# A graph layer on one Trainium2 core: one PSUM tile of two banks becomes two tiles of one bank each

## The chip, the cores and the metric

The kernel runs on one core of one Trainium2 chip. A core has five engines with an instruction queue each, and every queue is worked off in order: PE multiplies matrices (its weight loads are shown apart as PEld), DVE and ACT work element by element, POOL computes little here and issues the gathers, SP issues the other transfers. PE writes its results into PSUM, and DVE and ACT read and write there too. PSUM is divided into banks; the kernel counts a bank as 512 numbers of 32 bits in each of 128 partitions (P * G), and its PSUM tiles take eight banks in all. The engines wait for each other through semaphores. The metric is the time of one execution on the device in microseconds (us), as the median of several runs.

## What is computed

There are 12500 nodes of 128 features and 412500 edges, sorted by `dst`, one of them a loop from each node to itself.

```
theta = x[dst] - x[src]
w = sigmoid(relu(theta @ W1 + b1) @ W2 + b2)          # the gate: one number for each edge
agg = segment_sum(w * theta, dst)
indeg = segment_sum(1, dst)
out = layernorm(x + agg + indeg * (x @ W4 + b4))
```

## The kernel before, in words

**Table.** Since theta @ W1 is a difference of two rows of x @ W1, the kernel first makes a table `z` in device memory that holds x @ W1 and x for every node (`table_chunk`, lines 745 to 767). Each of 13 chunks has up to eight tiles of 128 nodes, worked in two halves of G = 4 tiles. For a half, PE transposes four tiles into PSUM (L754), ACT copies them to SBUF (L757), PE multiplies them by W1 (L760), ACT copies the product into the staged rows (L763). One PSUM tile `px` of two banks, from `wide()` (L737), takes both halves of a chunk, each half in a bank of its own.

**Parts.** The edges are worked in 276 parts of up to 1024 edges and more. Two parts make a block with one window of destination nodes. Parts from 18 on (PLAIN) run in a loop whose order is written out by hand for PE, DVE and ACT (`part`, under `manual_schedule`). For each part:

- POOL gathers the rows of `z` with eight indirect transfers (L395) into one of six buffers `zbuf`. The gather of part s + 3 is held until a matmul of part s - 1 is done, so at most some three parts lie ahead.
- PE spreads the rows of the destinations by a one-hot product into a PSUM tile `y` (L885, two buffers).
- DVE subtracts (L943), applies relu and W2 (L948), sums to the logits (L954) and makes one-hots (L918, L1122).
- ACT turns the logits into gates: L970 writes them into PSUM, L976 into SBUF. DVE weighs half of the rows with them at the start of the next part (L998), ACT weighs the other half (L1005).
- PE sums the weighed rows by destination (L1140). Every second part the sums of a block are completed (L1205) and normalised (L1233 to L1258).
- Edges whose source lies in 32 ranges of "hot" rows go another way: PE takes their rows from tables that stay in SBUF (L1059), makes their logits (L1086, L1087, L1100, the last into PSUM) and transposes them (L1103), ACT makes their gates and weighs them (L1092, L1109, L1112).

**Placement.** The lists of 64 parts (a set) are prepared during the parts before them, mostly on DVE. `place` (L498 to L709) is a generator of small steps, and `spend` gives each part a few of them, at the end of the part's DVE work. Named by what they do, they are: the start of a set (L527 to L545), 32 rounds of picking maxima (L573 to L580, all in SBUF), the hot list (L606, L612), four scans (L633 to L654), nine shifts (L671 to L674), and the end, which transposes the lists on PE and copies them on ACT (L694, L701, L705). The starts, hot lists, scans, shifts and ends need a PSUM scratch of up to one bank. One set is made before the loop and four in it; the last of these has only two parts, but its steps are the same.

**The tile that the change touches.** In the loop, one tile `px` of two banks lives from part 17 to the end. At part 17 it is cut in two by slices of one bank, `halves` (L1368, L1369): `halves[0]` is the placement's scratch, `halves[1]` holds the gates (`gate`, written by L970, read by L998), the hot edges' logits (`lgh`, written by L1100, read by L1109) and a node's own term (`own`, written by L1215, read and written by L1233). The kernel's language derives the semaphore waits from accesses to tiles. The same name `px` is used ahead of the loop for small tiles of `bases` (L432) and `first_turned` (L472), and for the placement's scratch while the first set is made.

Of the kernel before, what the change touches and what calls it, by code (L numbers as in the profile page):

```python
# [9 lines left out]
F32 = mybir.dt.float32  # L10
# [4 lines left out]
AF = mybir.ActivationFunctionType  # L15
# [5 lines left out]
P = 128  # L21
# [11 lines left out]
G = 4  # L33
# [49 lines left out]
def gnn_resnorm(  # L83
# [37 lines left out]
    nc = tc.nc  # L121
# [16 lines left out]
    while n0 < N:  # L138
        t = max(1, (N - n0) // P)
# [105 lines left out]
    ident = wni[:, 1, :]  # L245
# [35 lines left out]
    for i, t in enumerate(terms):  # L281
        at = slice(i * HALF // 2, i * HALF // 2 + 1)
# [141 lines left out]
    def bases(c0, c1, ps):  # L424

        b0, b1_ = c0 // SUB, c1 // SUB
        nc.vector.tensor_scalar(base_b[:, b0:b1_], base_r[:, c0:c1:SUB], float(N - WB), None,
                                op0=OP.min)
        nc.vector.tensor_scalar(first_b[:, c0:c1], base_r[:, c0:c1], float(N - SW), None,
                                op0=OP.min)  # L430
        nc.vector.tensor_copy(base_f[:, c0:c1], base_r[:, c0:c1])
        pb = ps.tile([P, 2 * P * G], F32, name="px")[:, :c1 - c0]  # L432
        nc.tensor.matmul(pb, ones_r, base_f[:, c0:c1], start=True, stop=True)
        first = first_c[:, c0:c1]
        nc.vector.tensor_copy(first, pb)
        for h in range(SUB):
            nc.vector.tensor_scalar(base_c[:, b0:b1_, h], first[:, ::SUB],
                                    float(N - WB), None, op0=OP.min)
        nc.vector.tensor_scalar(first, first, float(N - SW), None, op0=OP.min)
        lo = max(b0, 1)  # L440
        nc.vector.tensor_sub(step_c[:, lo:b1_], base_c[:, lo:b1_, 0], base_c[:, lo - 1:b1_ - 1, 0])
# [26 lines left out]
    def first_turned(t, ps):  # L468
        n = t.shape[0]
        f = turn_f[:n]  # L470
        nc.scalar.activation(f, t, AF.Copy)
        pt = ps.tile([P, 2 * P * G], F32, name="px")[:, :n]  # L472
        nc.tensor.transpose(pt, f, ident[:n, :n])
        return pt.rearrange("p (s k) -> p k s", k=K)

# [235 lines left out]
    with tc.manual_schedule(engines={SP}), tc.tile_pool(name="work", bufs=2) as wp, tc.tile_pool(  # L711
        name="ps_y", bufs=2, space=bass.MemoryType.PSUM
    ) as ps_y, tc.tile_pool(
        name="ps_l", bufs=1, space=bass.MemoryType.PSUM
# [7 lines left out]
        def next_xT():  # L722
            xTs.append(xT_buf[len(xTs) % len(xT_buf)])
            return xTs[-1]
# [5 lines left out]
        def y_tile():  # L730

            turn_y[0] += 1
            if turn_y[0] % 3 == 0:
                return pz.rearrange("p (g d) -> p g d", d=D)
            return ps_y.tile([P, G, D], F32, name="y")

        def wide():  # L737

            return ps_l.tile([P, 2 * P * G], F32, name="px")

        def turning():

# [2 lines left out]
        def table_chunk(c, xt):  # L745

            n0, np_, m = chunks[c]
            zt = staged[c % len(staged)]
            px = wide().rearrange("p (t e) -> p t e", e=P)
            for g0 in range(0, m, G):  # L750
                at = slice(g0, min(g0 + G, m))
                g = at.stop - g0
                for j in range(g0, at.stop):
                    pe = nc.tensor.transpose(px[:, j, :np_], xt[:np_, j, :], ident[:np_, :np_])  # L754
                table_steps.append(pe)
                xT = next_xT()
                nc.scalar.activation(xT[:, :g, :np_], px[:, at, :np_], AF.Copy)  # L757
                py = y_tile()[:np_, :g]
                for j in range(g):
                    pe = nc.tensor.matmul(py[:, j, :], xT[:, j, :np_], wts[:, 0, :],  # L760
                                          start=True, stop=True)
                table_steps.append(pe)
                nc.scalar.activation(zt[:np_, at, :D], py, AF.Copy)  # L763
            act = nc.scalar.activation(zt[:np_, :m, D:], xt[:np_, :m, :], AF.Copy)
            nc.sync.dma_start(
                z[n0:n0 + np_ * m, :].rearrange("(p t) d -> p t d", t=m), zt[:np_, :m, :])
            return pe, act
# [190 lines left out]
        halves = []  # L958
# [66 lines left out]
        def hot_load(f):  # L1025

            i0, g, i1, i = f
            a = i0
            while a < i1:
                (hot_s, _, n), j = hot_set(a)  # L1030
                m = min(i1 - a, n - j)
                nc.sync.dma_start(
                    hot_src[:, i % NU, (a - i0) * EP:(a - i0 + m) * EP],
                    hot_s[g, j:j + m].rearrange("(o p) l e -> o (p l e)", o=1).to_broadcast([P, m * EP]))
                a += m
# [40 lines left out]
        def tables():  # L1076

            for r in range(0, HR, RG):
                nc.sync.dma_start(
                    tabs[:, r:r + RG], x[r * HOT:(r + RG) * HOT, :].rearrange(  # L1080
                        "(r p t) d -> p r t d", p=P, t=HT))

        def hot_turned(t):

            xT = xT_all[:, (t - PLAIN) % HX, :]
            nc.tensor.matmul(pz, wneg, xT, start=True, stop=False)  # L1086
            nc.tensor.matmul(pz, y_of(t), blocks[t // SUB]["oh"][:, BP:], start=False, stop=True)  # L1087
# [174 lines left out]
        def fetch(b):  # L1262
            if b < NK:
                load_block(b)
# [73 lines left out]
        def spend(kinds, most=NS):  # L1338

            while most and credit[0] > 0 and steps[0] is not None and steps[1] in kinds:  # L1340
                credit[0] -= cost[steps[1]]
                advance(kinds)
                most -= 1

        def early_part(s):

            b, h = divmod(s, SUB)
            if s == 8:
                tables()
            credit[0] = min(credit[0] + 5.5, 5.5) if s < PLAIN - 5 else 200.0  # L1350
            if s == PLAIN - 4:
                credit[0] = 200.0
                spend("kspmcz")
                assert steps[0] is None
                credit[0] = 0.0
            for f in firsts.get(s, []) + [f for f in rest_of if max(f[0] - 7, PLAIN - 4) == s]:
                hot_load(f)
            if h == 0:
                if b + 2 >= NY:
                    fetch(b + 2)  # L1360
                if NY <= b + 1 < W0:
                    window(b + 1)
            elif b and b + 3 < PLAIN // SUB:
                load_dst(b + 3)
            while opened:
                hot_out(*opened.pop(0))
            if s == PLAIN - 1:
                px = wide()  # L1368
                halves.extend(px[:, i * P * G:(i + 1) * P * G] for i in range(2))  # L1369
                hot_turned(PLAIN)  # L1370
                hot_relu(PLAIN)
            if h and b:
                total(b - 1)
                own(b - 1)
            spend("c")
            logits(s)
            ends.append(newest[0])
            if s >= NH + 4:
                paced[s + AHEAD] = ends[-3]
            if s + AHEAD >= NH:  # L1380
                gather(s + AHEAD)
            if s + 1 < NH:
                parts[s + 1]["y"] = []
                spread_x(s + 1, 0, copied.pop())
                xT = copy_x(turn_x(s + 1, J))
                if s:
                    add_up(s - 1)
                spread_x(s + 1, J, xT)
                if s + 2 < NH:
                    px = turn_x(s + 2, 0)  # L1390
            else:
                for t in range(s + 1, s + 2 if s + 1 < PLAIN else s + 3):
                    spread_y(t)
                add_up(s - 1)
            if tiled:
                products_of_tiles()
            advance("p")
            gate_sums(s)
            weigh(s)
            if s + 2 < NH:  # L1400
                copied.append(copy_x(px))
            if s == PLAIN - 2:
                one_hot(PLAIN // SUB)
            if s == PLAIN - 1:
                one_hot(PLAIN // SUB + 1, 0, BP)
            if h:
                shift(b)
            if h == 0 and b > 1:
                normalize(b - 2)
            spend("ksmz")  # L1410
            if h == 0 and b + 1 < PLAIN // SUB:
                plain_one_hots(b + 1)
            if s - (PLAIN - 9) in range(len(OPENING)):
                tiles_of(groups[s - (PLAIN - 9)])
            fetch_step(s)
            if s == PLAIN - 1:
                hot_rows(PLAIN)
                hot_weights(PLAIN)

        ends = []  # L1420
        groups, firsts, i = [], {}, 0
# [118 lines left out]
    with tc.tile_pool(name="post_ps", bufs=1, space=bass.MemoryType.PSUM) as pps:  # L1540
        one = const.tile([P, 1], F32, name="one")
        nc.vector.tensor_reduce(one, bad, AX.X, OP.max)
        pb = pps.tile([P, P], F32, name="pb2")
# [193 lines left out]
```

## Time and profile before

| | |
|---|---|
| median of 3 runs (lowest to highest) | 3171.1 us (3168.46 to 3186.73) |
| the profiled execution's own time | 3168.71 us |
| its span, first to last instruction | 3166.6 us |
| PE, weight loads, DVE, ACT, POOL busy | 86%, 72%, 77%, 77%, 68% of the span |
| mean granted clock of PE | 0.889 |
| instructions | 53729 |

The profile is of one execution. A row of instructions gives the start in us from the start of the span, the time, the engine, the line of the kernel, the tile written and the tiles read, their shapes, and in brackets how long the engine had stood idle before it and what ended that. The waits are also given in sums: an engine and line, whom it waited for, us in total, how often, and the longest. A row of windows gives for a stretch of time its length, the busy time of each engine (with the number of instructions), the granted clock of PE (PEclk, 1.00 is full), the busy share of the DMA engines and GB/s.

### The profile page before, as it was taken

How to read it: one execution, taken by the hardware profiler on the slowest of the kernel's cores; microseconds unless marked ns; L12 is line 12 of the kernel's file. 1: busy time of each engine (PE TensorE's matmuls, PEld its weight loads, DVE VectorE, ACT ScalarE, POOL GpSimd, SP SyncE). 2: the span in 40 equal slices, each digit the busy share in tenths (PEclk: the TensorE clock that was granted, in tenths of full speed). 3: DMA queues.
4: the chain of work that ended last, by engine and by line, in shares of the span. 5: the costliest groups of instructions: out<-in, count | busy, mean ns of one | idle time of the engine just before them, and what ended most of it. 6: DMA issues, size and time to landing. Idle time of an engine off the chain costs nothing.

```text
span 3166.6 us, 53729 instructions
## 1 busy us (share of the span) xinstructions
PE 2736.3 (86%) x16422; PEld 2294.6 (72%) x16422; DVE 2435.9 (77%) x4150; ACT 2441.9 (77%) x6397; POOL 2157.0 (68%) x2213
## 2 busy tenths in 40 slices
PE   6868899998878999988798999888898999888797
PEld 5657677777767777767686777777677777777676
DVE  7998689887757988877557898877567888877555
ACT  5446888887767888876778898876787888877685
POOL 3674677777656777776566777776576777775573
PEclk7868899988888999988888999988898999988898
DMA  7564445554444555544354555454354555543342
GB/s 249 157 175 113 115 135 135 137 137 133 116 114 112 138 135 135 137 133 119 103 135 117 137 140 137 134 137 117 102 141 113 138 137 137 135 132 109 101 130 63
DMA packets 239303, 413.23 MB, mean 130 GB/s; under 512 B 63423, under 2 KB 147226, under 8 KB 237470
## 3 DMA queue, kind: packets, MB, share of 16 engines
q0 software_dynamic: 105280, 286.93, 33.0%
q1 hardware_dynamic: 131756, 116.40, 13.9%
q10 hardware_dynamic: 1970, 6.40, 0.6%
q8 instruction: 131, 2.15, 0.3%
q14 instruction: 166, 1.36, 0.1%
HBM read 388.57 MB, written 20.94 MB: 129 GB/s over the span
## 4 chain that ended last, share of the span: by engine, by line


## 5 line engine op out<-in xcount | busy, mean ns | idle before, releaser
L395 POOL DMA_INDIRECT zbuf<-z,src_i x2060 | 2007.3, 974 | 868.5 <-issue 385.4
L1059 PE MATMUL pd<-of,tabs 128*128 128x128 f32 (+2 forms) x4240 | 620.9, 310 | 0.0
L885 PEld LDWEIGHTS y<-y,oh 128*128 128x128 f32 (+1 forms) x2108 | 297.6, 212 | 426.1 <-DVE zbuf L943 359.5
L1059 PEld LDWEIGHTS pd<-of,tabs 128*128 128x128 f32 x4240 | 601.6, 227 | 0.0
L885 PE MATMUL y<-y,oh 128*128 128x128 f32 (+1 forms) x2108 | 328.8, 305 | 253.5 <-DVE zbuf L943 246.4
L1140 PE MATMUL pa<-wx,ow 128*104 128x260 f32 (+1 forms) x2284 | 534.9, 380 | 1.8 <-DVE wx L998 1.8
L1140 PEld LDWEIGHTS pa<-wx,ow 128*104 128x104 f32 x2284 | 369.6, 176 | 80.5 <-issue 2.9
L1092 ACT ACTIVATE hr<-pz 128x512 f32<-128x512 f32 x258 | 153.8, 596 | 314.7 <-PE pz L1087 314.6
L1100 PE MATMUL px<-w_c,hr 128*128 128x1 f32 x2064 | 302.5, 268 | 63.5 <-ACT hr L1092 58.9
L1100 PEld LDWEIGHTS px<-w_c,hr 128*128 128x128 f32 x2064 | 295.3, 220 | 79.5 <-ACT hr L1092 74.0
L1043 ACT ACTIVATE of<-hot_src,nodes 128x512 f32<-128x512 f16 (+2 forms) x530 | 344.4, 697 | 7.0 <-PE pd L1059 3.1
L948 DVE SCALAR_TENSOR_TENSOR zbuf<-zbuf,fix 128x1024 f32<-128x1024 f32 x273 | 331.6, 1215 | 9.3
L1112 ACT ACTIVATE wxh<-pz,wxh 128x128 f32<-128x128 f32 x1032 | 294.4, 368 | 53.0 <-PE pz L1103 48.4
L954 DVE TENSOR_REDUCE lg<-zbuf 128x8 f32<-128x1024 f32 x273 | 329.7, 1208 | 5.0
L1005 ACT ACTIVATE wx<-zbuf,wx 128x128 f32<-128x128 f32 x1028 | 328.7, 390 | 0.0
L943 DVE TENSOR_TENSOR zbuf<-y,zbuf 128x1024 f32<-128x1024 f32 x258 | 313.5, 1215 | 12.3 <-DMA zbuf<-z,src_i 12.2
L1045 ACT ACTIVATE of<-of 128x1024 f32<-128x1024 f32 (+1 forms) x265 | 274.2, 1035 | 8.4
L998 DVE TENSOR_TENSOR wx<-zbuf,px 128x512 f32<-128x512 f32 x258 | 175.9, 682 | 122.2 <-ACT px L970 60.1
L1086 PE MATMUL pz<-xT,wni 128*128 128x512 f32 x516 | 266.7, 599 | 1.1 <-ACT wxh L1112 1.1
L1087 PE MATMUL pz<-oh,y 128*128 128x512 f32 x516 | 267.2, 600 | 0.2 <-ACT oh L865 0.2
L1140 PE MATMUL pa<-wxh,owh 128*104 128x130 f32 x2064 | 262.2, 281 | 0.0
L1140 PEld LDWEIGHTS pa<-wxh,owh 128*104 128x104 f32 x2064 | 252.2, 178 | 0.0
(302 smaller groups left out, 4034.6 us busy)
## 6 DMA issues: line engine op xcount, KB each, us to landing
to_all<-off_d SPq DMA_DIRECT2D x258, 128.0 KB
zbuf<-z,src_i POOLq DMA_INDIRECT x2060
hot_src<-hot_s SPq DMA_DIRECT2D x228, 128.0 KB
z<-zbuf SPq DMA_DIRECT2D x10, 1024.0 KB
y<-z SPq DMA_DIRECT2D x270, 28.0 KB
xw<-in_x_dram SPq DMA_DIRECT2D x138, 52.0 KB
out_dram<-o SPq DMA_DIRECT2D x138, 52.0 KB
wx<-in_x_dram ACTq DMA_DIRECT2D x12, 512.0 KB
```

What stands on the lines that cost most here:

```text
L395: ins = nc.gpsimd.indirect_dma_start(out=rows_of(s)[:, k, :], out_offset=None, in_=z if s >= NH else x, in_offset=IndirectOffsetOnAxis(ap= ...
L885: nc.tensor.matmul(y[:, j, :], d["oh"][:, (k0 + j) * P:(k0 + j + 1) * P], y_of(s), start=True, stop=True)
L943: nc.vector.tensor_sub(half, yy.to_broadcast([P, 2, n, D]), half)
L948: nc.vector.scalar_tensor_tensor(h[:, at, :], h[:, at, :], 0.0, w2.to_broadcast([P, n, D]), op0=OP.max, op1=OP.mult)
L954: nc.vector.tensor_reduce(lg[:, at, 0], h[:, at, :], AX.X, OP.add)
L1005: nc.scalar.activation(wx[:, k, :D], rows_of(s)[:, k, D:], AF.Copy, scale=wx[:, k, D:D + 1])
L1043: nc.scalar.activation(of[:, t, :], hot_src[:, i % NU, :w], AF.Abs, bias=nodes[:, t:t + 1])
L1045: nc.scalar.activation(of, of, AF.Relu, scale=-1.0, bias=1.0)
L1059: newest[0] = nc.tensor.matmul(to[:, q], tabs[:, g * RG + q, t, :], of[:, t, q], start=t == 0, stop=t == HT - 1)
L1100: nc.tensor.matmul(lgh()[:, t % SUB, q:q + 1], hr[:, at], w2_c, start=True, stop=True)
L1112: nc.scalar.activation(wx[:, q, :D], pz[:, q * P:(q + 1) * P], AF.Copy, scale=wx[:, q, D:D + 1])
L1140: newest[0] = nc.tensor.matmul(to if len(w.shape) == 3 else to[:, 0, :], one, w, start=first and i == 0, stop=last and i == len(terms) - 1)
```

## The change

`px` is now a tile of one bank with two buffers, so the tiles take eight banks as before. In a table chunk each half takes its own tile, and in the loop the scratch and the gates' bank are two tiles. The small tiles of `bases` and `first_turned` follow.

```diff
@@ bases
-        pb = ps.tile([P, 2 * P * G], F32, name="px")[:, :c1 - c0]
+        pb = ps.tile([P, P * G], F32, name="px", bufs=2)[:, :c1 - c0]
@@ first_turned
-        pt = ps.tile([P, 2 * P * G], F32, name="px")[:, :n]
+        pt = ps.tile([P, P * G], F32, name="px", bufs=2)[:, :n]
@@ wide
-            return ps_l.tile([P, 2 * P * G], F32, name="px")
+            return ps_l.tile([P, P * G], F32, name="px", bufs=2)
@@ table_chunk
-            px = wide().rearrange("p (t e) -> p t e", e=P)
             for g0 in range(0, m, G):
+                px = wide().rearrange("p (t e) -> p t e", e=P)
                 at = slice(g0, min(g0 + G, m))
                 g = at.stop - g0
                 for j in range(g0, at.stop):
-                    pe = nc.tensor.transpose(px[:, j, :np_], xt[:np_, j, :], ident[:np_, :np_])
+                    pe = nc.tensor.transpose(px[:, j - g0, :np_], xt[:np_, j, :], ident[:np_, :np_])
                 table_steps.append(pe)
                 xT = next_xT()
-                nc.scalar.activation(xT[:, :g, :np_], px[:, at, :np_], AF.Copy)
+                nc.scalar.activation(xT[:, :g, :np_], px[:, :g, :np_], AF.Copy)
@@ early_part
             if s == PLAIN - 1:
-                px = wide()
-                halves.extend(px[:, i * P * G:(i + 1) * P * G] for i in range(2))
+                halves.extend(wide() for _ in range(2))
```

No instruction is added or removed. In the built programs the orders on POOL and SP are the same; on PE, DVE and ACT they differ only in the table and in the first set's placement, up to part 17, and agree from there to the end. What differs in the loop is which semaphores an instruction waits for. Before, the first scratch instruction of a scan or shift (L637 or L671) waits for the latest L1100 and L970, and L1233 or L998 behind an end of a set waits for L701 and L705. After, these waits are gone, and L998 or L1233 carries the wait for L1100 and L970 itself.

## The prediction

> **What bounds the kernel now.** I read the sums of waits first, since no engine is busy all the time, then windows of one block (two parts) in different stretches, then the rows of single parts. The windows show two kinds of block. The first row is a block while maxima are picked (only SBUF is used, I call it a picking block), the second a block while shifts are made (their scratch is in PSUM, a shifting block).
>
> ```profile
> 1142.00:1161.00 19.00, 17.98 (x121) 14.77 (x121) 17.99 (x30) 17.05 (x47) 14.43 (x16) 1.00 0.53 141
> 861.10:886.00 24.90, 20.79 (x113) 17.94 (x112) 18.56 (x31) 16.97 (x45) 15.13 (x16) 0.79 0.42 112
> ```
>
> A picking block takes some 18.9 us: PE is busy 17.98, DVE 17.99, ACT 17.05 of 19.0, so three engines together are its bound. A shifting block gives DVE almost the same work, 18.56, and takes about 24.9. PE's busy time is longer there only because its granted clock is 0.79 and not 1.00. So some 6 us of such a block are waits. The DVE rows of that block say which:
>
> ```profile
> 865.22 0.28 DVE L1205 TENSOR_TENSOR a<-a,pa 104x130 f32<-104x130 f32 x1
> 869.06 0.69 DVE L671 TENSOR_SCALAR px<-et 128x512 int32<-128x512 int32 x1 [3.55 <-ACT px L970]
> ...
> 872.16 0.45 DVE L674 COPY_PREDICATED ew<-px,et 128x255 f32<-128x255 int32 x1
> ...
> 874.02 0.68 DVE L998 TENSOR_TENSOR wx<-zbuf,px 128x512 f32<-128x512 f32 x1
> ...
> 881.85 0.69 DVE L671 TENSOR_SCALAR px<-ew 128x512 int32<-128x512 int32 x1 [2.20 <-ACT px L970]
> ```
>
> DVE has nothing to do until L970 has written the gates; only then comes the shift, 3.5 us (869.06 to 872.6), and only after it the weighing L998 and the next part's L943, for which PE's L885 waits (its tile `y` must be free). So the shift lies in a ring: L943, PE's L885 to L1103, ACT's L1109 to L970, shift, L998, L943. The shift writes the scratch and reads no gate. The wait for L970 comes from the common tile, not from data. In a picking block the same place holds 3.1 us of SBUF work that waits for nothing and runs while PE and ACT do their part of the ring.
>
> The idle PE costs more than the idle time:
>
> ```profile
> 2801.34 1.05 PE L885 MATMUL y<-y,oh 128*128 128x128 f32 x8
> ...
> 2803.58 1.95 PE L1059 MATMUL pd<-of,tabs 128*128 128x128 f32 x16
> ...
> 2813.70 2.07 PE L885 MATMUL y<-y,oh 128*128 128x128 f32 x8 [4.30 <-DVE zbuf L943]
> ...
> 2818.02 3.04 PE L1059 MATMUL pd<-of,tabs 128*128 128x128 f32 x16
> ```
>
> After 4.30 us of idling eight matmuls take 2.07 instead of 1.05 us, and sixteen later ones 3.04 instead of 1.95.
>
> **The change part by part.** Nothing is computed more or less, no transfer or gather is added, moved or resized, and the queues of SP and POOL keep their order. What changes is waits, in three places, and the order of the table.
>
> *(a) The scratch no longer waits for the gates.* The sums of DVE's waits give the price:
>
> ```profile
> DVE px L671 <- ACT px L970: 92.4, 33, 3.8
> DVE px L637 <- ACT px L970: 25.3, 11, 2.9
> DVE px L639 <- ACT px L970: 4.6, 4, 1.4
> ```
>
> A shift has 3.5 us of work to fill a wait of 2.8 us (92.4 / 33); only the longest, 3.8, leave 0.3 us over, for some 16 of the 33 (one per block): 92.4 - 16 x 0.3 = about 88. A scan has more than its wait behind L637:
>
> ```profile
> 2806.68 0.16 DVE L637 COPY px<-col 128x1 f32<-128x1 f32 x1 [2.93 <-ACT px L970]
> ...
> 2810.19 0.36 DVE L654 SCALAR_TENSOR_TENSOR ed<-ew,ed 128x192 int32<-128x192 int32 x1
> ```
>
> That is 3.9 us for a wait of 2.93, so 25.3 + 4.6 = 30 go whole (L639 still has to wait for the hot list's L612, which comes before L970 in ACT's order). Sum: 118. L998 and L1233 take over the wait for L970 as their own; behind them in DVE's queue stands L943, and for that PE's L885. What is late next: in the odd part L1233, which really reads what ACT's L1215 wrote, then PE and DVE together as in a picking block.
>
> As a second way, the four stretches with scans and shifts (7.5 blocks each), and a block in which ACT also makes the square root of the normalisation (every fifth):
>
> ```profile
> 727.90:911.30 183.40, 156.26 (x881) 134.88 (x882) 136.09 (x249) 130.85 (x340) 121.97 (x129) 0.83 0.46 124
> ...
> 2761.30:2947.80 186.50, 157.13 (x877) 135.79 (x878) 137.34 (x257) 129.41 (x340) 123.67 (x130) 0.83 0.44 122
> sum 735.60, PE 624.70 PEld 539.01 DVE 545.51 ACT 519.49 POOL 493.53; mean PE 156.18 PEld 134.75 DVE 136.38 ACT 129.87 POOL 123.38
> ```
>
> ```profile
> 1123.10:1146.70 23.60, 20.98 (x119) 17.72 (x118) 17.03 (x28) 20.07 (x50) 17.81 (x20) 0.86 0.50 136
> ```
>
> If DVE keeps its 136.4 and idles 1.0 per block as in the picking block (19.0 - 17.99), and 1.5 blocks of 7.5 pay 4.7 for the root (23.6 - 18.9), a stretch takes 136.4 + 7.5 + 7 = 151. Four of them: 604, which is 132 less than 735.6. I take the smaller, 118, since some of the waits hid the root. Ends: 60, if the clock does not come back (below), and 132.
>
> *(b) The end of a set and the hot list no longer hold the gates.* Here PE and ACT use the scratch, and DVE waits behind them:
>
> ```profile
> DVE wx L998 <- ACT rel L705: 37.7, 4, 11.3
> DVE px L1233 <- PE px L701: 35.4, 4, 9.2
> DVE wx L998 <- ACT src_i L705: 11.6, 4, 2.9
> DVE wx L998 <- ACT hrel L612: 10.3, 4, 3.4
> ```
>
> ```profile
> 925.14 0.75 PE L701 MATMUL px<-wni,es 128*128 128x128 f32 x4 [4.20 <-ACT es L694]
> ...
> 932.25 1.67 PE L885 MATMUL y<-y,oh 128*128 128x128 f32 x8 [3.09 <-DVE zbuf L943]
> ...
> 949.16 1.09 PE L885 MATMUL y<-y,oh 128*128 128x128 f32 x6 [3.51 <-DVE zbuf L943]
> ```
>
> DVE's 95 us are not all won. PE still stands 4.20 us before L701 until ACT's L694 is done, a real input, and DVE would idle beside that. What the ring gains is PE's wait at L885 after it, 3.09 + 3.51 = 6.6 per set, 26 for four; the hot lists give at most their 10.3, and I count 4. Together 30. Ends: 0, if PE is held anyway, and 60, halfway to DVE's sum.
>
> *(c) The table.* PE waits for ACT's copy between the halves; with both transposes issued first there is always a half to multiply:
>
> ```profile
> POOL zbuf L395 <- ACT src_i L705: 29.5, 1, 29.5
> ...
> PE y L760 <- ACT xT L757: 16.5, 17, 2.7
> ...
> PE pz L760 <- ACT xT L757: 5.8, 8, 1.3
> ```
>
> ```profile
> 160.00:180.00 20.00, 13.51 (x67) 12.43 (x66) 19.38 (x33) 4.26 (x15) 15.73 (x15) 0.59 1.06 330
> ```
>
> At most 16.5 + 5.8 = 22 us. But the loop starts when the first set's lists are there (POOL waits 29.5 for them), and DVE, which makes them, is busy 19.38 of 20 us after the table. A shorter table helps only as far as DVE's picking fits into it. The scheduler's order of the two also changes. I take 6, with -10 and 22 as ends.
>
> *Sum:* 118 + 30 + 6 = 154. The profiled execution took 3168.71, so 3015; the median, 3171.1, lies 2.4 above it: **3017 us**.
>
> [...] The gathers speak against more: POOL has little time to spare.
>
> ```profile
> L395 POOL DMA_INDIRECT zbuf<-z,src_i x2060 | 2007.3, 974 | 868.5 <-issue 385.4 <-PE pa L1140 221.8 <-DMA zbuf<-z,src_i 43.3
> ```
>
> ```profile
> L395 POOL DMA_INDIRECT zbuf<-z,src_i x178 | 178.8, 1004 | 54.2 <-issue 32.3 <-DMA zbuf<-z,src_i 4.0 <-ACT wx L1005 2.7
> ```
>
> ```profile
> L395 POOL DMA_INDIRECT zbuf<-z,src_i x73 | 69.0, 946 | 37.8 <-PE pa L1140 16.4 <-issue 14.6 <-ACT of L1043 1.5
> ```
>
> ```profile
> DVE zbuf L943 <- DMA zbuf<-z,src_i: 12.2, 13, 2.6
> ```
>
> The first row is the whole run, the second a stretch of picking (437 to 669 us), the third one of shifts (801.5 to 911.3). [...] If shifts packed more densely brought the picking's price, 60 parts of eight gathers would cost 480 x 58 ns = 28 us more of POOL's time, which counts only where POOL is the bound.
>
> [...]
>
> **The rivals.** *The gathers become the bound.* POOL's row has 868.5 us of idle time, of which 2060 x 0.30 = 618 lie between any two gathers; so 250 are waits, 221.8 of them for PE's L1140, which holds a gather that would run too far ahead.
>
> ```profile
> 2800.51 0.95 POOL L395 DMA_INDIRECT zbuf<-z,src_i  x1 [0.30 <-issue]
> ```
>
> ```profile
> L395 POOL DMA_INDIRECT zbuf<-z,src_i x2060: 940/946/1737, 278.7 to 3124.1; - x188
> ```
>
> DVE already waits 12.2 us for rows (L943, above). While maxima are picked, eight gathers take 8 x 1.304 = 10.4 us against the 9.45 of a part (18.9 / 2), and the lead melts; today the slow shifts refill it. At 1004 ns throughout, 2060 x 1.304 = 2686, after the start at 278.7 and with 41 from the last gather to the end (3166.6 - 3125): 3006 on the profile's scale, before any hold. If a fifth of the 221.8 stays, about 3045.
>
> *The clock does not come back.* Then each shifting block still pays (2.07 - 1.05) + (3.04 - 1.95) = 2.1 us on the two groups shown, and by my estimate 3 of its 6 with those between them. (a) falls to about 60, (b) to 20, and with (c) 86 remain: 3171 - 86 = 3085. Against it: picking blocks at 1.00 with PE 95% busy.
>
> *The idle time only moves.* DVE makes the shift early and then waits just as long before L998: 3150 to 3171. For it speaks that L998 waits for the same L970. Against it: in the block at 861 to 886 the 3.5 us of the shift lie between L970 and L943, with PE idle behind, so they are on the ring.
>
> *Slower.* The shifts now run while ACT and PE write other PSUM tiles more often. Should that slow them, a shifting block loses its gain when its two shifts grow from 7 to 13 us, a factor of 1.8, and the kernel is slower by 1% only above 2.1. So far the longest L671 took 695 ns:
>
> ```profile
> L671 DVE TENSOR_SCALAR px<-et x40: 426/559/695, 236.2 to 2931.4; 128x512 int32<-128x512 int32 x20, 128x255 int32<-128x255 int32 x20
> ```
>
> That is the 0.69 of 512 columns shown above, so none was slowed by what ran beside it.
>
> **How the numbers follow.** Forecast 0.60 (2990 to 3040); gathers 0.17 (3045); clock 0.10 (3085); only moved 0.08; slower 0.05. About 1%, 32 us, is what a measurement of this kernel can tell from no change. Faster by more: 0.60 + 0.17 + 0.10 = 0.87; within 1%: 0.08; slower: 0.05. The low end of the range takes the upper ends of the terms, 132 + 60 + 15 = 207: 2964. The high end, 3088, takes in gathers and clock and leaves out the last two cases and a little below.
>
> **What would show it.** The waits of L671 and L637 for L970 gone; L998 and L1233 waiting for L970 less in sum than before's L671, L637, L998 and L1233 together; shifting blocks at 19 to 20 us with PEclk near 1.00; L998 no longer behind L705; PE's waits for L757 gone and the lists of the first set up to 10 us earlier. Wrong would be: shifting blocks above 22 us; DVE waiting at L943 for the gathers by more than 40 us in sum, which means the gathers' rival; or a loop that starts later than before.

## The result, and the profile after

The changed kernel takes 2998.66 us (median of 4 runs, 2987.09 to 3005.32), the kernel before 3169.78 (4 runs, 3167.6 to 3186.73): a ratio of 0.945, with a 95% interval of 0.941 to 0.949, 171 us less. The forecast was 3017. The profiled execution is the shortest of the four (2987.09, span 2985.1), so differences between the two traces come out some 10 us larger than that of the medians (181.5 against 171.1).

The sums of waits of the changed kernel (engine and line, whom it waited for, us in total, times, longest):

```profile
DVE px L1233 <- ACT px L970: 143.0, 96, 4.3
PE y L885 <- DVE zbuf L943: 133.5, 123, 10.1
...
DVE wx L998 <- ACT px L970: 78.1, 44, 7.2
...
POOL zbuf L395 <- PE pa L1140: 42.7, 22, 10.9
...
PE px L701 <- ACT es L694: 22.5, 5, 5.7
...
DVE zbuf L943 <- DMA zbuf<-z,src_i: 19.6, 16, 3.7
...
PE y L760 <- ACT xT L757: 7.7, 7, 3.7
```

In the kernel before, three of these were:

```profile
PE y L885 <- DVE zbuf L943: 246.4, 128, 10.8
...
DVE px L1233 <- ACT px L970: 120.2, 81, 3.8
...
DVE wx L998 <- ACT px L970: 60.1, 39, 7.2
```

The waits of L671, L637 and L639 for L970 are gone, and so are those of L998 and L1233 for L705 and L701. L998 and L1233 wait more than before for L970, but DVE's waits for L970 fall in sum from 92.4 + 25.3 + 4.6 + 120.2 + 60.1 = 302.6 to 221.1. PE's wait ahead of L885, the other end of the ring, is almost halved.

A wait of the same kind is left inside the second tile: L1233 reads what L1215 wrote, and not the gates, but waits for L970. In these 96 waits L970 ends 0.2 to 0.3 us after L1215, 28.8 us in sum, so that is the most that a tile of its own for this term could take from the 143.0. It was not tried.

The windows of the four stretches with scans and shifts (length, then busy time of PE, PEld, DVE, ACT and POOL, PEclk, DMA share, GB/s), cut at the same parts as before; the first, the last and the sum:

```profile
711.50:862.00 150.50, 138.15 (x871) 114.29 (x870) 135.28 (x249) 131.71 (x346) 114.06 (x120) 0.95 0.52 142
...
2619.90:2777.70 157.80, 145.56 (x877) 122.11 (x876) 137.09 (x257) 132.94 (x350) 119.73 (x126) 0.90 0.52 139
sum 601.30, PE 552.92 PEld 458.64 DVE 541.75 ACT 525.80 POOL 455.70; mean PE 138.23 PEld 114.66 DVE 135.44 ACT 131.45 POOL 113.92
```

DVE's work is the same (541.75 us, before 545.51); the idle time beside it has gone. The three parts of the first end of a set, in the kernel before and in the changed one:

```profile
911.30:957.20 45.90, 35.09 (x180) 28.68 (x179) 19.33 (x34) 27.54 (x78) 22.69 (x24) 0.81 0.39 106
```

```profile
862.00:900.90 38.90, 34.69 (x214) 27.96 (x213) 19.28 (x33) 30.14 (x83) 29.34 (x31) 0.94 0.56 149
```

Cut in this way, at the starts of L943, the two spans compare as follows (us):

| | before | after | less |
|---|---|---|---|
| up to the loop's first L943 | 306.5 | 299.2 | 7.3 |
| four stretches of scans and shifts | 735.6 | 601.3 | 134.3 |
| four ends of sets, three parts each | 185.2 | 149.6 | 35.6 |
| two parts ahead of each stretch (hot list) | 101.7 | 84.9 | 16.8 |
| all the rest | 1837.6 | 1850.1 | -12.5 |
| span | 3166.6 | 2985.1 | 181.5 |

The rest has become longer. Two picking blocks of the changed kernel, with the same instructions, show how:

```profile
1654.70:1675.30 20.60, 19.58 (x119) 16.27 (x118) 17.94 (x29) 17.03 (x47) 15.75 (x16) 0.92 0.47 131
1843.60:1862.50 18.90, 17.88 (x119) 14.65 (x118) 17.82 (x29) 16.96 (x47) 14.63 (x15) 1.00 0.53 134
```

Of 51 blocks that pick maxima, place nothing else and have no root, 4 took 20.2 to 20.8 us before the change and 13 after it. What goes with this is in the last section.

### The profile page after: what moved, and what is told of

It is laid out like the page before. It is cut to its first block, busy times and chain, and to the rows that moved or that the text cites. A ratio compares the mean times of both kernels' runs of the same rounds, so it can differ in the third digit from the quotient of the medians.

```text
span 2985.1 us, 53729 instructions
## 1 busy us (share of the span) xinstructions
PE 2655.8 (89%) x16422; PEld 2212.0 (74%) x16422; DVE 2429.7 (81%) x4150; ACT 2437.2 (82%) x6397; POOL 2164.4 (73%) x2213
## 4 chain that ended last, share of the span: by engine, by line
## 5 line engine op out<-in xcount | busy, mean ns | idle before, releaser
L1059 PE MATMUL pd<-of,tabs 128*128 128x128 f32 (+2 forms) x4240 | 599.3, 303 | 0.0
L1059 PEld LDWEIGHTS pd<-of,tabs 128*128 128x128 f32 x4240 | 579.5, 219 | 0.0
L1140 PE MATMUL pa<-wx,ow 128*104 128x260 f32 (+1 forms) x2284 | 534.4, 379 | 1.8 <-DVE wx L998 1.8
L885 PEld LDWEIGHTS y<-y,oh 128*128 128x128 f32 (+1 forms) x2108 | 273.9, 196 | 312.1 <-DVE zbuf L943 243.1
L1140 PEld LDWEIGHTS pa<-wx,ow 128*104 128x104 f32 x2284 | 368.3, 176 | 81.4 <-issue 2.9
L885 PE MATMUL y<-y,oh 128*128 128x128 f32 (+1 forms) x2108 | 300.4, 287 | 141.3 <-DVE zbuf L943 133.5
L1100 PE MATMUL px<-w_c,hr 128*128 128x1 f32 x2064 | 284.6, 259 | 79.6 <-ACT hr L1092 75.0
L1043 ACT ACTIVATE of<-hot_src,nodes 128x512 f32<-128x512 f16 (+2 forms) x530 | 344.2, 696 | 3.9 <-PE pd L1059 0.8
L1100 PEld LDWEIGHTS px<-w_c,hr 128*128 128x128 f32 x2064 | 272.1, 205 | 99.2 <-ACT hr L1092 93.5
L943 DVE TENSOR_TENSOR zbuf<-y,zbuf 128x1024 f32<-128x1024 f32 x258 | 313.6, 1216 | 19.9 <-DMA zbuf<-z,src_i 19.6
L1005 ACT ACTIVATE wx<-zbuf,wx 128x128 f32<-128x128 f32 x1028 | 328.7, 390 | 0.0
L1087 PE MATMUL pz<-oh,y 128*128 128x512 f32 x516 | 267.2, 600 | 0.2 <-ACT oh L865 0.2
L1140 PE MATMUL pa<-wxh,owh 128*104 128x130 f32 x2064 | 255.8, 277 | 0.0
L1140 PEld LDWEIGHTS pa<-wxh,owh 128*104 128x104 f32 x2064 | 244.5, 173 | 0.0
L998 DVE TENSOR_TENSOR wx<-zbuf,px 128x512 f32<-128x512 f32 x258 | 175.9, 682 | 78.5 <-ACT px L970 78.1
```

Of the source, the lines that this page charges most:

```text
L885: nc.tensor.matmul(y[:, j, :], d["oh"][:, (k0 + j) * P:(k0 + j + 1) * P], y_of(s), start=True, stop=True)
L943: nc.vector.tensor_sub(half, yy.to_broadcast([P, 2, n, D]), half)
L1005: nc.scalar.activation(wx[:, k, :D], rows_of(s)[:, k, D:], AF.Copy, scale=wx[:, k, D:D + 1])
L1043: nc.scalar.activation(of[:, t, :], hot_src[:, i % NU, :w], AF.Abs, bias=nodes[:, t:t + 1])
L1059: newest[0] = nc.tensor.matmul(to[:, q], tabs[:, g * RG + q, t, :], of[:, t, q], start=t == 0, stop=t == HT - 1)
L1100: nc.tensor.matmul(lgh()[:, t % SUB, q:q + 1], hr[:, at], w2_c, start=True, stop=True)
```

## Experiments

The twelve runs fell on three chips. On that of e5 to e8 the kernel before takes 3166.95 us, as in the result. On the two of e1 to e4 and e9 to e12 it takes 3780.38 and 3780.71 us, and a picking block some 25 instead of 19. There ACT stands in most parts ahead of the instructions that read the loaded hot rows, here in e1 (its line of L1043):

```profile
ACT of L1055 <- remote: 598.6, 204, 5.0
```

"remote" means that the profile found no instruction for the event. On the other chip the same instruction has no such wait. The expectation of e5 takes it for hot rows that land late; the trace does not bear this out. Each of the 204 waits ends with an event of the one semaphore that PE's instructions raise, 1.5 to 4.6 us after the end of the last matmul before it that raises it. In e1 824 of this semaphore's 1520 recorded events come more than 0.5 us after such an end, in the trace after 2 of 1773. So on the slower chips ACT waits for word from PE that comes late, while PE has gone on to later matmuls; why it comes late the traces do not show. So a time is compared only with others of its own chip, and what a wait costs is read on e5 to e8.

**e5, the changed kernel again**

> The changed kernel unaltered, to stand on the same chip beside the next three. Where the chip is like the one of the result: ratio 0.945, 2999 us beside 3170. Where the kernel before takes some 3780 us, as on the chip of the first four experiments (ACT waits there some 600 us in sum for the hot rows to land, which the first chip did not show): the loads set the pace of a part, and the change is worth less, 0.97 to 0.98, somewhat below the ratio of 0.978 of the kernel in which scans and shifts wait.

Measured: 2985.95 us (2973.23 to 2991.32), ratio 0.941 (0.937 to 0.944), 181 us less than before. It is the measure for e6 to e8. Its loop starts at 297.2 us, its four stretches take 606.9, and DVE waits longer for gathered rows than in the first trace:

```profile
DVE zbuf L943 <- DMA zbuf<-z,src_i: 31.7, 29, 3.7
```

**e6 and e1, scans and shifts wait again**

`held` adds a wait for other instructions; the `memset` L639 of a first scan gets it too.

```diff
+    def held(ins, *others):
+        for other in others:
+            tc.add_manual_dep(ins.ins, other.ins.name, ...)
+        return ins
-                v.tensor_copy(odd[:, :1], c[:, 5:6])
+                held(v.tensor_copy(odd[:, :1], c[:, 5:6]), *gates)
-                v.tensor_scalar(bit, w[:, a:e], MOVES - r, 31, ...)
+                held(v.tensor_scalar(bit, w[:, a:e], MOVES - r, 31, ...), *gates)
-            nc.scalar.activation(filled(gate()...), ...)
+            gates[:] = [nc.scalar.activation(filled(gate()...), ...)]
```

> The kernel of e1 again, now beside the changed kernel on one chip. My theory (the wait of scratch for gates lies on the ring): 118 to 130 us more than the changed kernel where loads are not late. Rivals: no difference (the idle time only moves), or 60 to 90 (the gathers give part of it back).

Measured: 3099.42 us (3090.01 to 3111.2), ratio 0.979 (0.974 to 0.983), 113 us more than e5. The sums of waits of e6, where L671 is L682, L637 is L648 and L970 is L982, and the sum of its four stretches:

```profile
DVE px L682 <- ACT px L982: 89.9, 34, 3.8
...
DVE px L648 <- ACT px L982: 19.5, 11, 2.9
```

```profile
sum 716.70, PE 611.77 PEld 519.78 DVE 543.96 ACT 536.31 POOL 501.14; mean PE 152.94 PEld 129.95 DVE 135.99 ACT 134.08 POOL 125.28
```

The old waits are back (92.4 and 25.3 before), and the stretches are 110 us longer than in e5 (606.9). Nothing else was put back. So the wait for the neighbour in the tile was on the ring, and costs about what it lasts; "the idle time only moves" is refuted. The stretches of the kernel before are another 19 us longer (735.6), at a granted clock of 0.83 or 0.84 where e6 has 0.86 or 0.87; what makes this difference is not shown.

> The changed kernel, in which the first scratch instruction of every scan and shift again waits for the latest gates L970, as with one tile; nothing else is put back. My theory (the wait lies on the ring and was most of the gain): about 2999 + 118 = 3117 us, with shifting blocks at some 25 us and a granted clock near 0.8 in them. First rival (the idle time only moves between two waits of DVE): 2999, since L998 waits for L970 either way. Second rival (the gathers bound the changed kernel, so that time given back here is partly had again elsewhere): 3060 to 3090, with the picking blocks after the shifts shorter than in the changed kernel.

Measured, on a chip where the kernel before takes 3780 us: 3700.91 us, ratio 0.978 (0.973 to 0.982). With e3, below, at 3765.78 us, the other kind of wait is worth 65 us there. The size of this one can't be read there without the changed kernel beside it, but e2 against e3 gives some 20 us: where nearly every block takes 25 us for another reason, a late shift is mostly hidden.

**e7 and e2, waits at ends of sets and hot lists**

```diff
-            nc.vector.tensor_tensor(wx, xs, w.to_broadcast(list(xs.shape)), op=OP.mult)
+            held(nc.vector.tensor_tensor(wx, xs, w.to_broadcast(list(xs.shape)), op=OP.mult),
+                 *scratched.values())
...
-            nc.vector.tensor_sub(mine, mine, d["a"][:WB, :D])
+            held(nc.vector.tensor_sub(mine, mine, d["a"][:WB, :D]), *scratched.values())
...
-                    nc.tensor.transpose(pt[:, h, k, :], e[:, h, k * P:(k + 1) * P], ident)
+                    scratched["PE"] = held(nc.tensor.transpose(pt[:, h, k, :], ...), *gates)
...
+                if not q and copied_out:
+                    held(pe, copied_out.pop())
```

`scratched` holds the latest matmul and the latest copy on the scratch (L606, L701; L544, L612, L705), `copied_out` the latest L612 or L705, for which the first L1100 of a part waits; L612 and L705 wait for the latest L1239.

> The kernel of e2 again, beside the changed kernel on one chip: 30 us more than that by the sum of the prediction, 68 by the lengths of the parts in the two traces.

Measured: 3040.35 us (3036.9 to 3051.12), ratio 0.960 (0.956 to 0.964), 54 us more than e5. The waits that came back (L1233 is L1255, L998 L1015, L701 L715, L606 L617, L612 L624):

```profile
DVE px L1255 <- PE px L715: 35.8, 4, 9.1
...
DVE px L1255 <- PE px L617: 9.5, 3, 5.2
DVE wx L1015 <- ACT hrel L624: 9.3, 4, 2.6
```

The three parts of the four ends take 194.4 us, in e5 148.9; the two parts with a hot list 102.4 against 85.5. That is 62 us; in all the rest (the last row but one of the table) e7 is 12.5 us shorter than e5 (1838.3 against 1850.8), with 9 of the 51 picking blocks at 20.2 to 20.8 us and not 15. So the 54 us are a net sum. The second row, L1233 behind the hot list's matmuls on PE, is one that the prediction did not count. In the kernel before it was there under other names:

```profile
DVE px L1233 <- ACT wx L1005: 8.9, 2, 5.3
DVE px L1233 <- ACT of L1043: 7.1, 2, 3.6
...
DVE px L1233 <- PE px L606: 0.7, 1, 0.7
```

In all four sets L1233 starts there some 0.1 us after the last L606 ends; 3.55 us of the first row, the whole second and the third make 11.4 us.

> The changed kernel, in which the waits between gates and scratch that come from PE and ACT are put back: L998 or L1233 waits for the latest L606, L612, L544, L701, L705, L1100 for the latest L612 and L705, L606 and L701 for the latest L970. Scans and shifts stay free. By the sum of the prediction: 2999 + 30 = 3029 us. Rival, by the parts of the two traces (parts with an end of a set or a hot list were 52 + 16 us shorter after the change): 2999 + 68 = 3067.

Measured, on the slower chip: 3746.18 us, ratio 0.991 (0.988 to 0.994).

**e3 and e9, both kinds of wait, the table alone**

> Both kinds of wait put back: the loop waits as before the change, and only the table keeps its two tiles. By the sum of the prediction the table alone is worth 6 us: 3164 (ratio to before 0.998). If the three terms do not add up, it shows here against the two kernels with one kind of wait each: 3170 - 6 is to be 2999 plus their two losses.

Measured: 3765.78 us, ratio 0.994 (0.992 to 0.997).

> The kernel of e3 again (both kinds of wait put back, only the table's two tiles kept), on a chip where loads are not late if it falls on one. If the terms add up: 2986 + 113 + 54 = 3153 us, some 14 less than before, of which the earlier start of the loop (299.2 instead of 306.5 us) is 7. By the prediction's term for the table: 3167 - 6 = 3161. If the two kinds of wait cover each other, the kernel is slower than 3161 can tell: at or above before, 3167.

Measured: 3756.78 us, ratio 0.993 (0.991 to 0.995), again on a chip of the slower kind. There the table, its order and the small waits that e9 does not put back (such as 2.2 us of L539 for L970) are worth 15 to 24 us, more than forecast. On the chip of e5 the table was not measured alone; 181.0 - 113.5 - 54.4 leaves 13 us for it and for whatever does not add up, and the loop starts 7.3 us earlier in the profile (9.3 in that of e5).

**e8, PE kept busy while ACT makes the root**

```diff
+        def idle(n):
+            if steps[0] is None or picking[0]:
+                for _ in range(n):
+                    nc.tensor.matmul(halves[0][:, :P], ident, ident, start=True, stop=True)
...
             spread_ahead(s)
+            if h == 0:
+                idle(14 if rooted else 0)
             if t < NS:
                 hot_rows(t)
```

`picking` is true while maxima are picked.

> The changed kernel with extra work for PE in 17 of the blocks in which ACT makes the square root: fourteen 128x128 matmuls that nobody reads, into the scratch, ahead of L1100 in the even part, where PE stands some 2.1 us. No result changes. In the changed kernel such a block takes 23.6 us against 18.9; ACT's two table loads and the root are 2.9 us of it, and PE's slow stretch after the idle time takes the rest (L1100 1.86 instead of 1.0, L1059 3.6 instead of 1.95). Theory (idling lowers the clock): the slow stretch goes, 17 x 1.7 = 29 us less than the changed kernel. Rival (the clock falls for another reason, or PE's own time hides behind ACT there): no difference.

Measured: 2971.4 us (2965.86 to 2974.57), ratio 0.937 (0.934 to 0.940), 14.5 us less than e5 (0.5%; the highest run of e8 lies just above the lowest of e5). The same block in the changed kernel and in e8, as windows and as rows of PE (the 28 of L1477 are the filling's 14, L1104 is L1100, L1107 is L1103, L1063 is L1059):

```profile
548.40:572.00 23.60, 20.98 (x119) 17.77 (x118) 18.03 (x30) 19.96 (x49) 18.12 (x19) 0.86 0.49 130
```

```profile
552.91 1.86 PE L1100 MATMUL px<-w_c,hr 128*128 128x1 f32 x8 [2.10 <-ACT hr L1092]
554.63 1.09 PE L1103 MATMUL pz<-wni,xT 128*128 128x128 f32 x4
555.52 3.62 PE L1059 MATMUL pd<-of,tabs 128*128 128x128 f32 x16
```

```profile
552.30:573.70 21.40, 20.88 (x147) 17.70 (x146) 18.19 (x30) 20.02 (x50) 16.41 (x17) 1.00 0.47 131
```

```profile
554.61 3.29 PE L1477 MATMUL px<-wni 128*128 128x128 f32 x28
557.74 0.95 PE L1104 MATMUL px<-w_c,hr 128*128 128x1 f32 x8
558.55 0.63 PE L1107 MATMUL pz<-wni,xT 128*128 128x128 f32 x4
559.02 1.95 PE L1063 MATMUL pd<-of,tabs 128*128 128x128 f32 x16
```

Work that nobody needs makes the block 2.2 us shorter: the granted clock stays at 1.00, and L1059 takes 1.95 instead of 3.62 us. That is what the theory said: the 13 picking blocks with a root take 21.2 us on average, in e5 22.8, which is 22 us. The kernel gains only half of the 29 us. A part of what is missing is that more of the plain picking blocks then take 20.5 us (19 of 51, in e5 15), 5 us in sum in the two traces. By its median it beats both kernels.

**e4 and e11, PE kept busy in small waits**

```diff
+            if h == 0:
+                idle(3)
             spread_ahead(s)
+            if h == 0:
+                idle(3 if rooted else 3)
             if t < NS:
                 hot_rows(t)
```

`idle` is that of e8.

> The changed kernel with small extra work for PE: in even parts, while maxima are picked or nothing is placed (87 blocks), three 128x128 matmuls that nobody reads go into the scratch ahead of L885 and three ahead of L1100, where PE idles 0.52 and 0.51 us. No result changes. Theory (the 20.5 us blocks differ from the 18.9 us ones because this idle time falls such that a slow stretch of the clock repeats in every block): the blocks of 20.5 us become 18.9, some 15 x 1.6 = 24 us less, 2975 us. Rival (the slow stretch does not come from idling): no block gets shorter, and the kernel is the same or up to 87 x 0.3 = 26 us slower.

Measured: 3700.26 us, ratio 0.979 (0.974 to 0.984).

> The kernel of e4 again (three small matmuls for PE ahead of L885 and ahead of L1100 in 87 even parts, where PE idles 0.52 and 0.51 us; no result changes), on a chip where loads are not late if it falls on one. Theory (this idle time sets off the slow stretch of the clock in the blocks of 20.5 us): those become 18.9 us, 10 to 14 of them, 15 to 25 us less than the changed kernel. Rival (what sets it off is something else): no block is shorter, and the kernel is the same or some us slower.

Measured: 3696.3 us, ratio 0.978 (0.977 to 0.980). Both fell on the slower chips, where a picking block takes some 25 us with the filling too (25.2 in the one of e11 at 1400.0 us), so they tell nothing on the question; it stays untried where it matters.

**e10, seven of eight gathers**

```diff
-        for k in slots(s):
+        for k in list(slots(s))[:7 if s >= PLAIN else None]:
```

> The changed kernel without every part's last of eight gathers in the loop: the rows of one eighth of the edges are left out (what an earlier part left in the buffer is used), so POOL has 12% less to do, some 300 us. Rival of the prediction (the gathers are the bound now): at least 100 us less than the changed kernel, 2880 or lower. My theory (they bind only where DVE waits for them at L943, 19.6 us in sum after the change): 10 to 25 us less, some 2970.

Measured, on the slower chip: 3474.76 us, ratio 0.919 (0.917 to 0.920), where e11 on the same chip, which gathers all, has 0.978. So on that kind of chip an eighth of the gathers is worth some 220 us. By the sums it is not POOL's time that binds there, as the rival has it: POOL stands 543.1 us held by L1140 in e11 and 659.5 in e10. What falls with the gathers is ACT's wait ahead of L1043 for the late events of PE, from 641.7 to 54.1 us (e10 has 223.8 us more there by a row that names PE's L1087, e11 11.9), though 748 of 1550 recorded events are still late by more than 0.5 us; how the gathers act on it is not shown. On the chip of the result only the traces speak on the rival: DVE waits 19.6 us at L943, in e5 31.7.

**e12, two steps put off by one part**

```diff
         v.memset(left[:, HL:], 0.0)
+        yield "w"
...
         nc.scalar.activation(f, low, AF.Copy)
-        yield "p"
+        yield "w"
...
+                if steps[1] == "w" and now[0] is not None and since[0] == now[0]:
+                    return
```

> The changed kernel with the filling of e8, and two steps of the placement put off by one part, so that no engine stands behind an instruction that ACT has only just in its queue: DVE's L532 (it waits some 7 us for L527 in each set) and PE's L701 (4.2 us for L694). All results are the same. Theory (what is left of the loss in starts and ends of sets is waiting for ACT inside a part): 4 x (7 to 10) + 4 x 4 = 44 to 56 us less than the kernel of e8, 2915 to 2927. Rival (the part is bound by ACT there, which has 19 us of work in it): 10 us less or none.

Measured, on the slower chip: 3671.45 us, ratio 0.972 (0.971 to 0.974), 25 us less than e11 beside it. The two waits in e11 and in e12 (L532 is L534 and L535, L701 is L705 and L706):

```profile
DVE et L534 <- ACT et L529: 42.6, 5, 10.5
...
PE px L705 <- ACT es L698: 37.6, 5, 7.6
```

```profile
PE px L706 <- ACT es L699: 7.3, 1, 7.3
...
DVE et L535 <- ACT et L529: 4.4, 4, 1.2
```

Most of the waits go, as the theory said. How much of the 25 us is theirs and how much the other filling's is not separated, and on the chip of the result this kernel was not run.

## Why the prediction was right, step by step

- **The bound.** That the wait of scratch for gates lies on the ring L943, L885, L970, L998 is shown by e6: 113 us for waits of 89.9 + 19.5 = 109 (and 3.3 more at L639).
- **(a), 118 us.** Measured 113 by e6. The second way of working it out (a stretch of 151 us, four of them 604) is what the trace shows: 601.3 (606.9 in e5). Shifting blocks without a root take 19.9 us on average, forecast 19 to 20.
- **(b), 30 us.** Measured 54 by e7: the mechanism was right, the size too small. The step that failed is "the hot lists give at most their 10.3, and I count 4": those parts lost 16.8 us in the trace. The wait of L1233 for the matmuls of the hot list on PE, 11.4 us, was left out; its rows named mostly ACT's L1005 and L1043. For the ends I priced the ring by PE's wait at L885 alone, 26; the parts became 35.6 shorter, with PE's clock at 0.94 instead of 0.81. How much of that is the clock is not separated. PE's 4.20 before L701 stayed, as forecast (23.0 us in sum before, 22.5 after).
- **(c), 6 us.** The loop starts 7.3 us earlier; PE's waits for L757 fell from 16.5 + 5.8 to 7.7 + 4.3 and did not go.
- **The sum.** 154 forecast, 171 measured (181 in e5). In the two traces the stretches give 134.3 for the 118 of (a), ends and hot lists 52.4 for the 30 of (b), the start of the loop 7.3 for the 6 of (c), and the rest takes back 12.5, which was not foreseen. This last covers a part of what (a) and (b) fell short of, so that the forecast comes within 18 us is partly luck.
- **Two slips in the working.** The gathers' rival adds up to 3006 + 44 = 3050, not 3045, and the low end of the range takes 15 for (c), whose upper end was 22. Neither changes the forecast.
- **The rivals.** *Gathers:* the hold of POOL by L1140 fell from 223.0 to 42.7, so most of its spare time was used up as feared, but DVE waits 19.6 us for rows (31.7 in e5), below the 40 that I named as the sign. It comes close. The denser shifts did not bring the price of picking, 1004 ns: a gather takes 951 to 956 ns on average in the four stretches, before 949 in the first and 951 in the last. On the slower chips the gathers matter, but not through POOL's time (e10). *The clock does not come back:* in part. It is 0.90 to 0.98 in the four stretches (0.83 or 0.84 before), and a quarter of the picking blocks is slowed, 0.92 in the one shown. That a picking block's small waits leave the clock alone, as the prediction took it from blocks at 1.00, does not hold. *The idle time only moves:* refuted by e6 and by the 302.6 and 221.1 us. *Slower scratch:* the longest L671 takes 0.696 us, before 0.695:

```profile
L671 DVE TENSOR_SCALAR px<-et x40: 422/557/696, 231.7 to 2763.3; 128x512 int32<-128x512 int32 x20, 128x255 int32<-128x255 int32 x20
```

## What to carry to other kernels

A tile that is shared for room carried waits here as one thing, whichever slice was touched (L671 waited 92.4 us for L970, which writes the other half): where two users of one tile sit on different engines, look in the sums of waits for a reader that waits for a writer of data it never reads. Such a wait cost about its whole length here where the work behind it lies between two steps of a ring that carries from one round of the loop to the next (113 us for waits of 113), and less where something else set the pace (some 20 us on the slower chip). When a wait goes, count every pair of users of the tile, not only those whose rows are large: a wait can be booked under another releaser, as that of L1233 for L606 was.

## What the runs showed of the hardware that was not expected

**A step that is a quarter idle can be followed by half of PE's clock.** In the traces before and after, the granted clock reads 1.00 or 0.50 and nothing else, and it keeps one value for 3.413 us or a whole multiple of that: so do 177 of 178 stretches before and 149 of 150 after, all but the last of each trace. Cut into steps of this length at its changes, the two picking blocks shown above read, first the one of 20.6 us:

```profile
1655.16:1658.58 3.42, 2.40 (x17) 1.87 (x17) 3.39 (x4) 3.36 (x7) 2.66 (x3) 1.00 0.61 150
1658.58:1661.99 3.41, 3.41 (x18) 3.41 (x18) 3.31 (x7) 2.75 (x12) 2.65 (x3) 0.50 0.69 194
1661.99:1665.40 3.41, 3.41 (x29) 3.21 (x28) 3.38 (x4) 3.38 (x8) 2.60 (x3) 1.00 0.49 140
```

```profile
1842.90:1846.31 3.41, 2.59 (x12) 1.33 (x10) 3.38 (x5) 3.38 (x7) 2.50 (x4) 1.00 0.52 138
1846.31:1849.72 3.41, 3.21 (x29) 3.21 (x30) 3.38 (x6) 3.20 (x12) 2.50 (x4) 1.00 0.62 164
```

In the first block both small waits of PE (ahead of L885 and of L1100) fall into one step, 1.02 of 3.42 us idle, and the next step has half the clock. In the second block 0.82 fall into it, the second wait reaches over its end, and the clock stays. Over the whole trace after, with PE counted as idle where neither a matmul nor a weight load runs, a step at full clock was followed by one at half so often:

| idle share of the step | steps | followed by half the clock |
|---|---|---|
| under 24% | 606 | 1 |
| 24 to 30% | 43 | 21 |
| 30 to 50% | 27 | 8 |
| over 50% | 51 | 45 |

So between a quarter and a half something else decides too, which the traces do not show. From half back to full it went after 71 of 95 steps with under 2% idle, and after 3 of 49 with more. That filling a wait keeps the clock up is shown by e8 for a wait of 2.1 us (1.00 and not 0.86 in the block shown there); for the small waits it was not tried on this chip. The rows suggest that the pace of a block is a matter of phase: 18.9 us are 5.5 steps, so the waits fall differently each time, while a slowed block of 20.5 us is 6.0 steps. Of the slowed blocks in this trace seven are followed at once by another plain picking block, and all seven of these take 20.5 us again (5 of 7 in e5).

**Chips differ.** The same kernel takes 3167 us on one chip and 3780 on two others, 19% more. DVE and ACT have about the same work there (2437 and 2468 us in e9, 2436 and 2442 in the trace before). What differs in the traces is that the events of PE's semaphore come late: more than 0.5 us after the end of the last matmul that raises it in 824 of 1520 cases in e1, and in 2 of 1784 in the trace before. ACT's stop at L1043, what the gathers cost (e10) and the small worth of the shifts' wait go together with that; what delays the events stays open.
